# First block's way to its experts on VectorE, second block's front in the head, and a new order table

## The chip, the cores and the metric

The kernel runs on one core of a Trainium2 chip. The time is device microseconds of one execution of the whole program; a median of three runs stands for a kernel. The engines are called as in the profile: PE (matrix products, with PEld for its weight loads), DVE (VectorE), ACT (ScalarE), POOL (GpSimd) and SP, which issues most of the transfers. Each engine works through its own queue in order, and semaphores make it wait for the others.

## The reference

Input is x of 4 sequences with 512 tokens of 256 numbers. Two layers follow, each as x + layernorm(f(layernorm(x))). All numbers are float32.

```python
def _mamba_forward(hidden_states, in_proj_w, conv_w, conv_b, x_proj_w, dt_proj_w, dt_proj_b, A, D, out_proj_w):
    proj = jnp.einsum('bld,ed->ble', hidden_states, in_proj_w)
    x, gate = jnp.split(proj, 2, axis=-1)
    ...
    xc = jax.nn.silu(xc + conv_b[None, :, None])
    ...
    dt = jax.nn.softplus(dt + dt_proj_b)
    def step(state, inp):
        dt_t, x_t, B_t, C_t = inp
        dA = jnp.exp(dt_t[..., None] * A)
        dBx = dt_t[..., None] * B_t[:, None, :] * x_t[..., None]
        state = state * dA + dBx
        y = jnp.einsum('bds,bs->bd', state, C_t)
        return (state, y)
    ...
    y = ys.transpose(1, 0, 2) + xt * D
    y = y * jax.nn.silu(gate)
    return jnp.einsum('bld,ed->ble', y, out_proj_w)
...
    probs = jax.nn.softmax(xt @ w_router, axis=-1)
    top_w, top_i = jax.lax.top_k(probs, TOP_K)
    ...
    g = jax.nn.silu(jnp.einsum('td,edh->teh', xt, we1)) * jnp.einsum('td,edh->teh', xt, we3)
    g = g * cw[:, :, None]
    moe_out = jnp.einsum('teh,ehd->td', g, we2)
    shared = jax.nn.silu(xt @ ws1) * (xt @ ws3) @ ws2
    out = shared / (k + 1) + moe_out * (k / (k + 1))
```

The inner width is 512 with 16 states for each channel; there are 16 experts of width 128, 4 of which are chosen for each token, and a shared one of width 512. All 16 are computed for every token and weighted with `cw`, which is zero for those not chosen.

## The kernel before

The 2048 tokens are cut into 8 blocks of 256 (`N`, `U`); two blocks make a sequence, so an odd block takes over the convolution's tail (`tails`) and the scan's state (`carry`) of the block before it. Each block goes through four stages.

- **front** (L655): statistics of x on DVE (`stats`), 1/deviation on POOL (`rstd`, four small instructions, L380 to L387), normalisation on ACT (`norm`), transposes on PE, copy out of PSUM on ACT (`evict`, giving `xn_t`), the in-projection in two halves (`in`), its copy into a padded tile on ACT (`pad`, with POOL's `pad0` for the three columns before it), the convolution on PE, `sigmoid` on ACT, `silu` on DVE, `x_proj`, `dt`, `softplus`, the products `inputs` on POOL, the gate, and transfers through memory (`rep`, `xg`, `bc`) that spread the results over partitions.
- **scans** (L820): 32 slots for each block (`SLOTS`). A slot is `exps` on ACT (L529), for two slots one `dbx` on POOL (L541), the `scan` on DVE (L824), the product with C on DVE (`hc`, L832), and for four slots one `sum` on PE (L846). After every eight slots `close` (DVE, L858) adds the skip term, and `yg` (POOL, L864) applies the gate. There are three buffers each of `h` (the scan's tile, in PSUM) and `dbx`.
- **chain** (L918): the block's way to its experts: `out0` and `out` (out-projection on PE, L941), `stats1` (DVE), `rstd1` (POOL), `norm1` (ACT), `add1` (POOL, the residual sum, L957), `stats2` (DVE), `rstd2` (POOL), `norm2` (ACT), `turn2` (PE transposes), `evict2` (ACT copy, L974), then the router and the choice of experts.
- **experts** (L1129): ten batches of two experts; the shared one makes the first two. A batch is `h1` and `h3` on PE (L1088, 8 instructions each), `act` on ACT, `gated` on DVE (L1107), `weighted` (L1103, not for the shared one) and `product` (L1110) on POOL, and `down` on PE (L1123). The first may start when `evict2` of its block is done. `fin` to `fstore` normalise, add the residual and store; the last block does it in two halves from PSUM, with the subtraction and the sum on DVE (L1201, L1206).

Block 0's front is written out in `first()` (L545), the head, in a fixed order, while the weights arrive. Idle PE time there is filled with matmuls of the identity (`warm`), which compute nothing. Everything else is a list of tasks, each with its engine, an assumed duration and a rank. `Plan.order()` (L212) makes one order of them by a simulation in which the task with the lowest rank among those that can start is taken next; ranks come from the block and slot, and are moved by the tables `SHIFTS`, `PATIENCE` and `NUDGES`. The order fixes each engine's queue. Where it expects PE to be idle before the first `down`, it puts in `warm` matmuls too. These are the lines of the chain that the change replaces for block 0:

```python
        step("stats1", "DVE", 0.6, stats1, [own("out")], [("mv", own("mv1"))], [own("c1")])
        step("rstd1", "POOL", 1.3, lambda: rstd1(4 * EPS), [own("stats1")], [("rstd", own("rstd1"))], [own("mv1")])
        step("norm1", "ACT", 0.92, norm1, [own("rstd1")], [("o", own("o"))], [own("c1"), own("rstd1")])
        step("add1", "POOL", 1.23, add1, [own("norm1"), own("xr")], (), [own("o"), own("xr")])
        step("stats2", "DVE", 0.615, stats2, [own("add1")], [("mv", own("mv2"))], [own("xr")])
        step("rstd2", "POOL", 1.39, lambda: rstd1(EPS), [own("stats2")], [("rstd", own("rstd2"))], [own("mv2")])
        step("norm2", "ACT", 1.0, norm2, [own("rstd2")], [("xn2", own("xn2"))], [own("xr"), own("rstd2")])
```

Of the kernel before, what the change touches and what calls it, by code (L numbers as in the profile page):

```python
# [57 lines left out]
    fA=(-2, -14.75, -1.5, -59.5, 52, 5.75, 37.75, 15),  # L58
    fB=(20.5, -5, 12.5, 6.25, 26.25, 45.25, 0, -46),
    fC=(7.75, 2, -31, -1.5, 13.5, 14, -33.5, 18),  # L60
    fD=(12, 34.75, 16.5, 0.25, -2.5, 39.25, 8, 11.25),
    exps=(5.75, 36.5, 17.25, -3.75, -60, 51.75, 2, 37.75),
    dbx=(6.5, 1.25, -27.75, -13.5, -14.25, 5.25, 14.25, 46.5),
    scan=(33.75, 18.75, -5.75, 40.75, 52.75, 51.5, 57.25, -15.75),
    hc=(-4.75, -60, 50.25, -27, 28.5, 59.25, 16.75, 26.75),
    keep=(58, 0, -5.75, 0, 52, 0, 14.5, 0),
    sum=(60, -12.75, 1.25, 31.25, 16.5, 7, 0.5, -43.25),
    close=(-4.75, 27.5, 5.5, -13.75, -3, 20, 15, 36.5),
    ld=(1.5, 29.25, 27, -3, 15.75, -7.5, 57.5, -5.25),
    bc=(5, 3, 5.25, 6, 10.5, 15.75, 0.75, -3.25),  # L70
    chain=(-26, -5.25, -55, -60, -6, -38.25, -22.75, 0.25),
    load=(-5.5, 34, -50.25, 21.25, -21.25, -44, 2.75, 5.5),
    h1=(45.5, 3, -35.75, 8.25, 25.75, -0.5, 14.75, 34.5),
    h3=(11.25, -3, -53.5, -26, -29.25, -19, -15.75, -4),
    act=(-6.25, 40.25, 5.5, -11.5, -31.5, 0, 0, -3.25),
    gated=(-2, -9.5, -4.5, -23.25, 11.75, -60, -3, 0),
    prod=(33, -50, 58.75, -60, -50.75, -26.25, -8.75, 0),
    down=(-18.75, 25.5, -45, 42.25, -60, -14, 0.75, 37),
    fin=(14.75, -3, 27.75, 59, 0.5, 59.5, 3.5, -4),
# [3 lines left out]
    fA=(1.5, 0.1, 0.1, 0.3, 0.1, 1, 0.3, 0.1),  # L83
    fB=(2.2, 0.1, 0.1, 0.3, 0.1, 2.2, 0.6, 0.6),
    fC=(0.3, 0.1, 0.3, 1, 0.1, 0.6, 0.3, 0.3),
    fD=(2.2, 0.1, 0.1, 0.1, 0.1, 0.1, 0.1, 0.6),
    exps=(0.1, 0.1, 0.6, 0.1, 1.5, 0.3, 1.5, 0.3),
    dbx=(0.1, 0.3, 0.1, 0.1, 0.1, 0.1, 1, 1.5),
    scan=(0.1, 0.1, 0.1, 0.6, 0.1, 0.1, 0.1, 0.1),
    hc=(0.1, 0.1, 0.6, 1.5, 2.2, 0.1, 2.2, 0.1),  # L90
    keep=(0.1, 0.1, 0.1, 0.1, 0.6, 0.1, 0.1, 0.1),
    sum=(2.2, 0.1, 0.1, 0.1, 2.2, 0.1, 0.1, 0.1),
    close=(0.1, 0.1, 0.6, 1, 0.3, 0.3, 0.6, 1.5),
    ld=(1.5, 0.3, 1.5, 0.3, 0.1, 0.1, 0.1, 1.5),
    bc=(0.6, 0.1, 0.1, 1, 1, 0.1, 0.1, 0.3),
    chain=(0.6, 0.6, 0.1, 0.6, 0.6, 1, 0.1, 2.2),
    load=(2.2, 1, 0.6, 1, 2.2, 2.2, 0.6, 0.1),
    h1=(0.3, 0.3, 0.3, 0.1, 0.1, 0.1, 0.3, 0.1),
    h3=(0.1, 0.3, 2.2, 0.1, 0.1, 1, 0.6, 0.1),
    act=(0.6, 2.2, 0.1, 0.3, 0.1, 0.1, 0.6, 2.2),  # L100
    gated=(0.6, 0.3, 1, 0.1, 0.6, 0.1, 0.1, 1),
    prod=(2.2, 0.1, 0.1, 0.1, 0.1, 0.3, 0.1, 1.5),
    down=(0.1, 0.1, 0.1, 1.5, 0.1, 0.3, 0.1, 0.3),
    fin=(0.3, 0.3, 0.1, 1.5, 0.1, 1, 1, 0.3),
# [3 lines left out]
    ("gin", 0, 0): 5.5, ("pad0", 1, 0): 5.75, ("in", 1, 0): 3, ("xg", 1, 0, 1): 8,  # L108
    ("inputs", 1, 0): 8, ("gate", 1, 0): 14.5, ("evict", 2): 16.5, ("conv", 2, 1): -5.5,
# [41 lines left out]
    close=(CI, "close yg"),  # L151
    ld=(CI, "reps loadxg decay0 decay1 delta"),
    bc=(1, "bc"),
    chain=(1, "xr out0 out stats1 rstd1 norm1 add1 stats2 rstd2 norm2 turn2 evict2 router pads logits "
           "exp choose chosen total share turnw weigh store_cw"),
    load=(NB, "w13 w2 cwb"),
    h1=(NB, "h1"),
# [1168 lines left out]
```

## Time and profile before

| | us |
|---|---|
| median of 3 runs | 694.24 (693.81 to 694.54) |
| the profiled execution | 694.61 |
| its span in the profile | 692.5 |
| busy: PE, DVE, ACT, POOL | 675.8, 578.2, 493.2, 601.6 |
| first scan, last scan ends | 27.89, 613.41 |
| first expert matmul, last `down` ends | 120.16, 687.51 |
| warming matmuls of the order, 164 between 28.0 and 119.9, busy | 21.00 |

The span runs from the program's first instruction to its last; some 2 us of the execution lie around it. Times in views are counted from the start of the span. The first column of a timeline is the start, the second the duration; a bracket tells how long the engine was idle before, and who ended that.

### The profile page before, as it was taken

What the parts mean: (1) busy time and instruction counts of PE and PEld (TensorE: products, weight loads), DVE (VectorE), ACT (ScalarE), POOL (GpSimd) and SP (SyncE); (2) the same over time, 40 slices, a digit from 0 to 9 for tenths busy, and PEclk for the clock granted to TensorE, in tenths of its full rate; (3) what the DMA queues carried; (4) which work ended last, traced back from release to release, by engine and by line L of the source; (5) the groups of instructions that cost most, each with busy time, mean ns of one, the idle gap of its engine ahead of it and who ended that gap; (6) DMA issues with size and microseconds to landing.
All of it is one profiled execution on the core that took longest, in us unless ns stands there. A gap on an engine that the chain in (4) does not pass through costs nothing.

```text
span 692.5 us, 13366 instructions
## 1 busy us (share of the span) xinstructions
PE 675.8 (98%) x4480; PEld 539.9 (78%) x4480; DVE 578.2 (83%) x821; ACT 493.2 (71%) x1308; POOL 601.6 (87%) x607
## 2 busy tenths in 40 slices
PE   8999998999999999999999999999999999999997
PEld 7777776767878678877787787787877787888886
DVE  3698999999999899999999999889999979952112
ACT  2799979988778778877798857877778657733311
POOL 1598669999999999999999999999999999985553
PEclk9999999999999999999999999999999999999999
DMA  5396775586876586788668766688767756464560
GB/s 175 114 352 227 258 238 188 188 270 202 288 230 226 208 307 207 233 264 285 211 227 281 244 221 229 213 290 286 246 240 232 237 190 213 140 227 128 191 229 31
DMA packets 84840, 155.28 MB, mean 224 GB/s; under 512 B 9858, under 2 KB 33410, under 8 KB 84772
## 3 DMA queue, kind: packets, MB, share of 16 engines
q1 hardware_dynamic: 83940, 153.13, 66.3%
q10 hardware_dynamic: 832, 1.31, 0.5%
q8 instruction: 35, 0.57, 0.3%
q14 instruction: 33, 0.27, 0.1%
HBM read 135.40 MB, written 19.01 MB: 223 GB/s over the span
## 4 chain that ended last, share of the span: by engine, by line
PE 62%; DVE 13%; ACT 10%; POOL 8%; DMA 3%; issue 3%; SPq 0%; DVEq 0%; POOLq 0%
PE h L1088 30%; PE po L1123 14%; DVE h L824 7%; PE y L846 6%; POOL dbx L541 4%; ACT h L529 4%; DVE hc L832 3%; PE f L941 3%; PE f L427 2%; PE f L442 2%; DMA xg<-gate 1%; PE f L1123 1%; PE f L349 1%; DVE gate L786 1%; POOL g L1110 1%
## 5 line engine op out<-in xcount | busy, mean ns | idle before, releaser
L824 DVE TENSOR_TENSOR_SCAN h<-h,dbx 128x512 f32<-128x512 f32 x256 | 307.5, 1220 | 11.5 <-ACT h L532 5.9
L541 POOL TENSOR_TENSOR dbx<-rep,bt 128x1024 f32<-128x1024 f32 x127 | 299.7, 2362 | 12.8 <-DVE h L824 12.5
L1088 PE MATMUL h<-xn_t,w 128*128 128x256 f32 x1280 | 295.2, 382 | 0.1
L529 ACT ACTIVATE h<-rep,a_rep 128x256 f32<-128x256 f32 x512 | 244.6, 478 | 53.4 <-DVE hc L832 41.8
L1088 PEld LDWEIGHTS h<-xn_t,w 128*128 128x128 f32 x1280 | 239.5, 190 | 42.7 <-issue 4.0
L832 DVE TENSOR_TENSOR hc<-h,ct 128x512 f32<-128x512 f32 x256 | 170.2, 682 | 2.9 <-ACT carry L836 0.7
L1123 PE MATMUL po<-w,g 128*128 128x256 f32 x600 | 143.6, 382 | 0.8 <-POOL g L1110 0.8
L1123 PEld LDWEIGHTS po<-w,g 128*128 128x128 f32 x600 | 111.8, 190 | 22.0 <-POOL g L1110 3.2
L1110 POOL TENSOR_TENSOR g<-g,q 128x512 f32<-128x512 f32 x80 | 101.6, 1270 | 9.1 <-DVE q L1107 7.1
L1107 DVE SCALAR_TENSOR_TENSOR q<-th,h 128x512 f32<-128x512 f32 x80 | 54.4, 681 | 49.5 <-PE h L1088 41.6
L1103 POOL TENSOR_TENSOR g<-g,cwb 128x512 f32<-128x512 f32 x64 | 81.4, 1271 | 14.6 <-ACT g L1100 13.9
L1095 ACT ACTIVATE th<-h 128x512 f32<-128x512 f32 x80 | 47.5, 594 | 46.8 <-PE h L1088 46.6
L846 PE MATMUL y<-hc,sel 128*32 128x256 f32 x1024 | 67.7, 385 | 0.0
L846 PEld LDWEIGHTS y<-hc,sel 128*32 128x32 f32 x1024 | 27.4, 109 | 28.6 <-issue 14.5
L532 ACT COPY h<-zero 128x1 f32<-128x1 f32 x256 | 41.7, 163 | 8.2
L427 PE MATMUL f<-xn_t,w_in 128*128 128x256 f32 x176 | 42.5, 384 | 1.6 <-DVE gate L786 1.1
L1100 ACT COPY g<-h 128x512 f32<-128x512 f32 x64 | 37.1, 580 | 8.7 <-PE f L1123 8.7
L427 PEld LDWEIGHTS f<-xn_t,w_in 128*128 128x128 f32 x176 | 32.7, 190 | 9.1 <-DVE gate L786 1.7
L836 ACT COPY carry<-h 128x2 f32<-128x2 f32 x128 | 19.6, 159 | 15.4 <-DVE hc L832 7.7
L442 PE MATMUL h<-xp,taps 64*64 64x256 f32 x288 | 29.5, 381 | 0.8 <-DVE xt L459 0.8
L941 PE MATMUL f<-w_out,yg 128*128 128x256 f32 x112 | 26.7, 384 | 0.3 <-DVE xt L459 0.3
L442 PE MATMUL f<-xp,taps 64*64 64x256 f32 x208 | 25.3, 382 | 0.7 <-DVE gate L786 0.4
(178 smaller groups left out, 631.2 us busy)
## 6 DMA issues: line engine op xcount, KB each, us to landing
w<-in_w SPq DMA_DIRECT2D x80, 512.0 KB, 4.4
rep<-rep SPq DMA_DIRECT2D x124, 256.0 KB, 4.6
w<-in_w SPq DMA_DIRECT2D x80, 256.0 KB, 4.5
cwb<-cwd SPq DMA_DIRECT2D x64, 256.0 KB, 5.1
xg<-xg SPq DMA_DIRECT2D x32, 256.0 KB, 4.5
bt<-bc SPq DMA_DIRECT2D x8, 512.0 KB, 5.8
ct<-bc SPq DMA_DIRECT2D x8, 512.0 KB, 6.1
xg<-gate SPq DMA_DIRECT2D x16, 256.0 KB, 4.6
```

Of the source, the lines that this page charges most:

```text
L427: T.matmul(t[:, j, :], w_in[:, k, ts(2 * m + j, P)], q["xn_t", n][:, k, :], start=k == 0, stop=k == CD - 1,)
L442: T.matmul(t[j][half[r ^ j], :], taps[half[r], 2 * m + j, k, :], q["pad", n, m][half[r], j, k : k + U], start=k == 0, stop=k == KC - 1,)
L529: S.activation(h[:, j, :], dt[:, m, 0, :], AF.Exp, scale=a_rep[:, c, g, m : m + 1])
L541: G.tensor_tensor(t[:, m], reps[n * CI + c][:, m, 1, :], bt[:, m], ALU.mult)
L824: V.tensor_tensor_scan(flat, flat, dbx[:, ts(p, NJ), :].rearrange("p j t -> p (j t)"), 0.0, ALU.mult, ALU.add)
L832: V.tensor_tensor(hc, expo[k], ct, ALU.mult)
L846: T.matmul(ys[n, c][m * CS : (m + 1) * CS, :], sel, hcs[k][:, j, :], start=g == 0, stop=g == SG - 1,)
L1088: T.matmul(t[:, j, :], weights[i][:, j, ts(CD * w + k, P)], x[:, k, :], start=k == 0, stop=k == CD - 1,)
L1103: G.tensor_tensor(gs[i], gs[i], cws[i], ALU.mult)
L1107: V.scalar_tensor_tensor(t, hid[i, "th"], 1.0, hid[i, 1], ALU.add, ALU.mult)
L1110: G.tensor_tensor(gs[i], gs[i], hid[i, "q"], ALU.mult)
L1123: T.matmul(acc[n][t] if n == N - 1 else acc[n][:, t, :], gs[i][:, j, ts(t, P)], weights2[i][:, j, :], start=m == 0 and j == 0 and (t == 0 ...
```

## The change

The diff has four parts. Block 0's `close` of the last eight slots leaves its result in PSUM and its `yg` is done on DVE (`quick`). Block 0's chain from `stats1` to `norm2` uses a shorter form: DVE makes the variance plus epsilon beside the statistics (`spread_of`), POOL does the power alone, DVE subtracts the mean in PSUM (`mean1`), scales and adds the residual in one instruction for each half (`scaled1`), and normalises (`scaled2`). The head takes over block 1's front up to the first half of its in-projection, its padding columns, and block 2's statistics; x(1) is asked for earlier, and some of the head's warming matmuls give way to these matmuls. All three tables hold other numbers (only the row of the chain is shown).

```diff
@@ -55,86 +55,83 @@
 SHIFTS = dict(
...
-    chain=(-26, -5.25, -55, -60, -6, -38.25, -22.75, 0.25),
...
+    chain=(-44.5, -50.5, -41.75, -50.75, 13, -21.25, -59.75, -15),
...
@@ -308,6 +305,7 @@
     nc.sync.dma_start(out=chan, in_=a["chan"].rearrange("(c p) k -> p c k", p=P))
+    load_x(1)
     w_x = const.tile([P, CI, P // 2], F32, name="w_x")
@@ -326,8 +324,7 @@
     nc.sync.dma_start(out=bsel, in_=a["bsel"])
-    for n in range(1, 3):
-        load_x(n)
+    load_x(2)
     w_out = const.tile([P, CI, D], F32, name="w_out")
@@ -420,14 +417,20 @@
 
-    def in_proj(n, m, bank):
-        t = q["in", n, m] = ps.tile([P, 2, U], F32, name=bank)
+    def in_parts(n, m, t):
+        q["in", n, m] = t
         for j in range(2):
             for k in range(CD):
                 T.matmul(
                     t[:, j, :], w_in[:, k, ts(2 * m + j, P)], q["xn_t", n][:, k, :],
                     start=k == 0, stop=k == CD - 1,
                 )
+                yield
+    def in_proj(n, m, bank):
+        for _ in in_parts(n, m, ps.tile([P, 2, U], F32, name=bank)):
+            pass
 
@@ -553,6 +556,8 @@
                 xn[:, i, :], xs[0][:, i, :], st[:, i, 1:2], rstd[:, i : i + 1],
                 ALU.subtract, ALU.mult,
             )
+        mr = rstd_of(stats_of(xs[1]))
         xn_t = q["xn_t", 0] = ring(work, [P, CD, U], "xn_t")
         for k, nm in enumerate(("f", "h1")):
             t = ps.tile([P, U], F32, name=nm)
@@ -560,6 +565,8 @@
         make_taps()
+        xn1 = ring(work, [P, NU, D], "o")
+        normalize(xn1, tiles_of(xs[1]), mr)
         for m in range(2):
@@ -571,8 +578,15 @@
             conv(0, m, (("po", "f"), ("h1", "h3"))[m])
+        t = ps_e.tile([P, CD, U], F32, name="h")
+        for k in range(CD):
+            for i in range(NU):
+                T.transpose(t[:, k, ts(i, P)], xn1[:, i, ts(k, P)], ident)
         sigmoid(0, 0)
         silu(0, 0)
+        q["xn_t", 1] = ring(work, [P, CD, U], "g")
+        V.tensor_copy(q["xn_t", 1], t)
 
@@ -580,8 +594,22 @@
         silu(0, 1)
+        live[2]["mv"] = stats_of(xs[2])
+        parts = in_parts(1, 0, ps_e.tile([P, 2, U], F32, name="h"))
+        for m in range(2):
+            xp = q["pad", 1, m] = ring(work, [P, 2, KC - 1 + U], "xp")
+            G.tensor_copy(xp[:, :, 0 : KC - 1], tails.pop((1, m)))
+        def some(c):
+            if c == 1:
+                next(parts)
+                next(parts)
+            else:
+                warm(2, "f")
         S.activation(spare, zero, AF.Softplus)
-        x_proj(0, "y", lambda c: warm(5 - c, "f"))
+        x_proj(0, "y", some)
         ssm(0)
@@ -592,7 +620,9 @@
         V.tensor_copy(first_b, b0)
-        warm(2, "y")
+        for _ in parts:
+            pass
+        V.tensor_copy(q["pad", 1, 0][:, :, KC - 1 :], q["in", 1, 0])
         softplus(0)
@@ -642,6 +672,10 @@
             (), (), [("xt", 0, m)], 256)
+    did(("evict", 1), [("g", ("xn_t", 1))], eng="DVE")
+    for m in range(2):
+        did(("pad0", 1, m), [("xp", ("xp", 1, m))], [("tail", 1, m)], eng="POOL")
+    did(("tail", 1, 0), (), [("xp", 1, 0)], eng="DVE")
     did(("bc", 0), [("bt", ("bt", 0)), ("ct", ("ct", 0))])
@@ -679,12 +713,12 @@
 
-        if n:
+        if n > 1:
             if n > 2:
                 once(key("x"), "SP", 0.5, lambda: load_x(n), (), [("x", key("x"))], (), 256)
 
             def stats():
-                mine["mv"] = stats_of(xs[n])
+                mine["mv"] = live[n].get("mv") or stats_of(xs[n])
 
@@ -714,6 +748,8 @@
 
+        if n:
             def pad0(m):
@@ -727,12 +763,13 @@
 
-            for m in range(2):
+            for m in range(n == 1, 2):
                 ends = (n + 1) % UB
                 starts = n % UB
-                once(key("pad0", m), "POOL", 0.12, lambda m=m: pad0(m),
-                     [("tail", n - 1, m)] if starts else [], [("xp", key("xp", m))],
-                     [("tail", n, m)] if starts else [])
+                if n > 1:
+                    once(key("pad0", m), "POOL", 0.12, lambda m=m: pad0(m),
+                         [("tail", n - 1, m)] if starts else [], [("xp", key("xp", m))],
+                         [("tail", n, m)] if starts else [])
                 banked(key("in", m), 1.73, lambda m=m: in_proj(n, m, bank_of(m)), [key("evict"), key("pad0", m)],
@@ -852,16 +889,25 @@
 
+    def quick(n, c=CI - 1):
+        return n == 0 and c == CI - 1
     def close(n, c):
 
         xg = xgs[n * CI + c]
-        V.scalar_tensor_tensor(xg[:, 0, :], xg[:, 0, :], d_skip[c], ys[n, c], ALU.mult, ALU.add)
+        to = ys[n, c] if quick(n, c) else xg[:, 0, :]
+        V.scalar_tensor_tensor(to, xg[:, 0, :], d_skip[c], ys[n, c], ALU.mult, ALU.add)
 
     def gated_y(n, c):
         xg = xgs[n * CI + c]
         if c % 2 == 0:
             ygs[n, c // 2] = ring(work, [P, 2, U], "yg")
-        G.tensor_tensor(ygs[n, c // 2][:, c % 2, :], xg[:, 0, :], xg[:, 1, :], ALU.mult)
+        if quick(n, c):
+            V.tensor_tensor(ygs[n, c // 2][:, c % 2, :], ys[n, c], xg[:, 1, :], ALU.mult)
+        else:
+            G.tensor_tensor(ygs[n, c // 2][:, c % 2, :], xg[:, 0, :], xg[:, 1, :], ALU.mult)
 
@@ -909,9 +955,10 @@
                     [("sum", s), ("loadxg", i)], (), [("y", i), ("xgt", i)])
-                add(("yg", i), "POOL", 0.685, k - 3 if last else k + 3, lambda n=n, c=c: gated_y(n, c),
+                fast = quick(n, c)
+                add(("yg", i), "DVE" if fast else "POOL", 0.385 if fast else 0.685, k - 3 if last else k + 3, lambda n=n, c=c: gated_y(n, c),
                     [("close", i)] + ([("yg", i - 1)] if i else []),
-                    [("yg", ("yg", n, c // 2))] if c % 2 == 0 else [], [("xgt", i), ("yg", n, c // 2)])
+                    [("yg", ("yg", n, c // 2))] if c % 2 == 0 else [], [("xgt", i), ("yg", n, c // 2)] + ([("y", i)] if fast else []))
 
@@ -925,7 +972,7 @@
             count[0] += 1
-            prev = [(nm, n - 1)] if n else []
+            prev = [(nm, n - 1)] if (nm, n - 1) in plan.names else []
             add((nm, n), eng, dur, base + 0.05 * count[0], fn, list(deps) + prev, alloc, uses, kb)
@@ -948,6 +995,37 @@
             z["mr"] = rstd_of(z["mv"], eps)
+        def spread_of(t):
+            st = z["mv"] = stats_of(t)
+            z["rstd"] = stat.tile([P, NU], F32, name="rstd")
+            V.tensor_scalar(
+                z["rstd"], st[:, :, 2], 1.0 / D, 4 * EPS if t is z["o"] else EPS, ALU.mult, ALU.add
+            )
+        def power():
+            G.tensor_tensor(z["rstd"], z["rstd"], mhalf, ALU.pow)
+        def mean1():
+            for i in range(NU):
+                V.tensor_scalar(z["o"][:, i, :], z["o"][:, i, :], z["mv"][:, i, 1:2], None, ALU.subtract)
+        def scaled1():
+            for i in range(NU):
+                V.scalar_tensor_tensor(
+                    xr[n][:, i, :], z["o"][:, i, :], z["rstd"][:, i : i + 1], xr[n][:, i, :],
+                    ALU.mult, ALU.add,
+                )
+        def scaled2():
+            z["xn"] = ring(work, [P, NU, D], "xn2")
+            for i in range(NU):
+                V.tensor_scalar(
+                    z["xn"][:, i, :], xr[n][:, i, :], z["mv"][:, i, 1:2], z["rstd"][:, i : i + 1],
+                    ALU.subtract, ALU.mult,
+                )
 
@@ -1041,13 +1119,26 @@
              [("yg", n, 1), own("c1")])
-        step("stats1", "DVE", 0.6, stats1, [own("out")], [("mv", own("mv1"))], [own("c1")])
-        step("rstd1", "POOL", 1.3, lambda: rstd1(4 * EPS), [own("stats1")], [("rstd", own("rstd1"))], [own("mv1")])
-        step("norm1", "ACT", 0.92, norm1, [own("rstd1")], [("o", own("o"))], [own("c1"), own("rstd1")])
-        step("add1", "POOL", 1.23, add1, [own("norm1"), own("xr")], (), [own("o"), own("xr")])
-        step("stats2", "DVE", 0.615, stats2, [own("add1")], [("mv", own("mv2"))], [own("xr")])
-        step("rstd2", "POOL", 1.39, lambda: rstd1(EPS), [own("stats2")], [("rstd", own("rstd2"))], [own("mv2")])
-        step("norm2", "ACT", 1.0, norm2, [own("rstd2")], [("xn2", own("xn2"))], [own("xr"), own("rstd2")])
+        if quick(n):
+            step("stats1", "DVE", 0.75, lambda: spread_of(z["o"]), [own("out")],
+                 [("mv", own("mv1")), ("rstd", own("rstd1"))], [own("c1")])
+            step("rstd1", "POOL", 0.71, power, [own("stats1")], (), [own("rstd1")])
+            step("mean1", "DVE", 0.9, mean1, [own("stats1")], (), [own("c1"), own("mv1")])
+            step("add1", "DVE", 0.9, scaled1, [own("rstd1"), own("mean1"), own("xr")], (),
+                 [own("c1"), own("rstd1"), own("xr")])
+            step("stats2", "DVE", 0.75, lambda: spread_of(xr[n]), [own("add1")],
+                 [("mv", own("mv2")), ("rstd", own("rstd2"))], [own("xr")])
+            step("rstd2", "POOL", 0.71, power, [own("stats2")], (), [own("rstd2")])
+            step("norm2", "DVE", 0.75, scaled2, [own("rstd2")], [("xn2", own("xn2"))],
+                 [own("xr"), own("rstd2"), own("mv2")])
+        else:
+            step("stats1", "DVE", 0.6, stats1, [own("out")], [("mv", own("mv1"))], [own("c1")])
+            step("rstd1", "POOL", 1.3, lambda: rstd1(4 * EPS), [own("stats1")], [("rstd", own("rstd1"))], [own("mv1")])
+            step("norm1", "ACT", 0.92, norm1, [own("rstd1")], [("o", own("o"))], [own("c1"), own("rstd1")])
+            step("add1", "POOL", 1.23, add1, [own("norm1"), own("xr")], (), [own("o"), own("xr")])
+            step("stats2", "DVE", 0.615, stats2, [own("add1")], [("mv", own("mv2"))], [own("xr")])
+            step("rstd2", "POOL", 1.39, lambda: rstd1(EPS), [own("stats2")], [("rstd", own("rstd2"))], [own("mv2")])
+            step("norm2", "ACT", 1.0, norm2, [own("rstd2")], [("xn2", own("xn2"))], [own("xr"), own("rstd2")])
         step("turn2", "PE", 0.46, transpose, [own("norm2")],
```

## The prediction

> **What bounds the kernel now.** I read the busy time by stretches first, then the first block's way to its experts in the order of time, then the last block's. The first view gives busy time of PE, PEld, DVE, ACT and POOL in four stretches: the first block's scans, its way to the experts, the long middle until the last scan ends at 613.4, and the rest.
>
> ```profile
> core 0: us, PE busy (x) PEld busy (x) DVE busy (x) ACT busy (x) POOL busy (x), PEclk, DMA share, GB/s
> 28.00:99.00 71.00, 66.58 (x641) 51.50 (x640) 68.36 (x89) 62.09 (x179) 56.26 (x56) 1.00 0.75 250
> 99.00:120.00 21.00, 18.42 (x132) 14.56 (x130) 19.75 (x27) 18.85 (x48) 18.62 (x28) 1.00 0.64 226
> 120.00:613.40 493.40, 490.88 (x3143) 388.26 (x3142) 461.55 (x634) 381.20 (x1024) 479.81 (x460) 1.00 0.71 236
> 613.40:692.50 79.10, 74.11 (x373) 63.84 (x371) 17.04 (x39) 19.09 (x37) 42.58 (x52) 0.98 0.45 151
> ```
>
> Up to 99 DVE sets the pace (96% busy; POOL 79%). In the middle POOL is fullest: 479.81 of 493.40 is 97.2%, idle 13.6 us; DVE 93.5%, idle 31.9 us. PE's 490.88 overstates it, since a matmul of 256 columns is shown as 379 ns but a run of 8 in the chain takes 1.73 us, 216 ns each. After 613.4 only PE matters. So there are two accounts: the last scan's end, which DVE and POOL set, and PE's expert work, which can only begin when the first block has reached its experts.
>
> Block 0's way, instructions in order of time (start, duration):
>
> ```profile
> 99.10 0.47 DVE L858 SCALAR_TENSOR_TENSOR xg<-xg,chan,y 128x256 f32<-128x256 f32 x1
> ...
> 99.64 0.73 POOL L864 TENSOR_TENSOR yg<-xg 128x256 f32<-128x256 f32 x1
> ...
> 102.92 0.69 DVE L377 BATCH_NORM_STATS2 st<-h 128x6 f32<-128x512 f32 x1
> ...
> 105.41 2.35 POOL L541 TENSOR_TENSOR dbx<-rep,bt 128x1024 f32<-128x1024 f32 x1
> 105.75 1.01 ACT L391 ACTIVATE o<-h,off,rstd 128x256 f32<-128x256 f32 x2
> ...
> 107.99 1.28 POOL L957 TENSOR_TENSOR xr<-xr,o 128x512 f32<-128x512 f32 x1
> ...
> 113.61 0.71 POOL L385 TENSOR_TENSOR rstd<-rstd,mhalf 128x2 f32<-128x2 f32 x1
> ...
> 117.71 0.58 ACT L974 COPY xn_t<-h 128x512 f32<-128x512 f32 x1
> ```
>
> From the close at 99.10 to the end of the copy that experts read, 118.29, is 19.2 us; about 7.7 of it is waiting: `add1` sits behind a `dbx` of 2.35, `rstd2` behind a `dbx` and a `u` (110.00 to 113.16). The first expert matmul is at 120.16.
>
> The last block's way:
>
> ```profile
> 618.40 0.48 DVE L858 SCALAR_TENSOR_TENSOR xg<-xg,chan,y 128x256 f32<-128x256 f32 x1 [2.82 <-PE y L846]
> ...
> 631.38 0.59 ACT L974 COPY xn_t<-f 128x512 f32<-128x512 f32 x1
> ...
> 637.27 1.89 PE L1123 MATMUL po<-w,g 128*128 128x256 f32 x8
> ```
>
> At 631.97, when block 7's experts may begin, PE has of block 6 only the rest of one `down` (1.2 us) and one whole (1.73): 2.9 us. So PE can arrive at most 2.9 us earlier before it waits for the last scans; more must come from a sooner end of the scans.
>
> **The head.** Added on DVE: statistics of x(1) and x(2), 0.69 each (L377), and two copies of 128x512 from PSUM, 0.69 each (L569 on DVE). On POOL four small ones, 0.19+0.22+0.71+0.20 = 1.3, and two tail copies of 0.19. On ACT two normalisations, 1.1. On PE four transposes, 0.55, and `in` of block 1, 1.73, for 4+2 warming matmuls. Covers: ACT stood idle 2.08 before 11.81; POOL stood idle 15.5 before 22.92; DVE 3.4 before 22.41 (x(2) statistics) and 1.2 before 24.07 (the pad copy). Without its cover each would cost its own length. Not covered is the copy of `xn_t` 1: it stands on DVE between the two `silu`, which run without a gap (16.95 to 19.01). It pushes the second by 0.69; the matmuls behind started at 19.34 though their data was there by 18.6 and 19.0, so 0.3 is absorbed: **+0.4 us**, bounds 0 and 0.8.
>
> x(1) is now asked for behind `chan`, at about 1.6 on SP's queue, not 8.03; w_x, one_row, w_dt, a_rep, rsel and bsel move back by one issue and 256 KB. Its statistics are ahead of DVE's copy of `xn_t` 0 at 9.57, so a late landing would hold the head. w_x, issued at that very place, landed at 8.02, and x(1) is wanted at 8.1; it is twice the bytes in half as many rows. I take 0, keep 1.5 us as the upper bound. w_x is wanted only at 17.49.
>
> **Block 0's scans.** Two statistics leave DVE (one stood at 27.27, straight before the first scan): -1.4. With the head +0.4 the close comes 1.0 earlier. POOL loses rstd of block 1 and two pads, 1.3+0.4; ACT normalisation, copy and pad, 2.3; PE 2.3.
>
> **The way itself.** Work, by rows: close 0.40 (pipelined), `yg` on DVE 0.45 (nearest L858), out 1.56, statistics 0.69 and a 128x2 step 0.17 (nearest the reciprocal, 166 ns), power on POOL 0.71, subtraction of the mean beside it, scale and add 0.87 (the pair L1206 at 688.87 to 689.74), statistics and step 0.86, power 0.71, two normalising steps 0.74 (L552), transposes 0.55, copy 0.58: 8.6, and nine crossings of some 0.1: 9.5. Waits that the row cannot show: power behind a `dbx` 0 to 2.36, twice; four times a scan of 1.22 ahead on DVE; once exps on ACT, 0 to 1. Together 0 to 10.6. I take 3.0, nearer the low end, because a power of 0.71 has two small gaps to hit where before three POOL steps had to be fitted. Way: **12.5 instead of 19.2, -6.7** (bounds -9.7 and +0.9). Experts begin 7.7 earlier.
>
> DVE pays for it: 0.45 + 2x0.17 + mean 0.85 (pair L1201) + 0.87 + 0.74 = 3.25, and behind them in its queue stand block 1's scans, for which exps and `dbx` buffers wait. POOL sheds yg 0.73, add 1.27, six small ones 1.2: 3.2. ACT sheds 2.1.
>
> The Trainium skill, "SBUF — State Buffer", Who interferes with whom, speaks against the last of these steps: a `tensor_scalar` from SBUF to SBUF may take a two-port mode, and then DVE and GpSimd lock each other out for a whole instruction. L552, which has that form, ran at 410 ns beside an idle POOL, so no row here shows the lock; by the rule one step could wait for a whole `dbx`, the way would be 2.4 longer, and PE's account below would give 2.6 and bind: 691.6.
>
> **PE's account.** Experts 7.7 earlier; but in 110.4 to 118.3 PE did real work of two `in` (3.46), transposes 0.55 and one `sum` 1.0, some 5.0, which is now later; 2.3 went into the head. 7.7 - 5.0 + 2.3 = 5.0 earlier, if nothing else binds.
>
> **The scans' end.** By POOL: 3.2 + 1.7 less work, +0.4: -4.5. By DVE: +3.25 - 1.4 + 0.4: +2.3. POOL is the fuller in the middle, but DVE before it; two thirds to one: **-2.3**. Of the 2.9 us left over one `down` goes: **-1.7**. Sum **-4.0**. PE's 5.0 allows it.
>
> **The new table** changes every engine's order. Seven blocks of 32 scans with nearly the same work started 71.5, 73.0, 76.2, 75.2, 74.6, 70.6 and 75.0 us apart (standard deviation 2.1); over seven independent ones that is 2.1 x 2.65 = 5.5. I take 0 for it and keep 5.5 both ways.
>
> The span was 692.5 and that execution 694.61, 0.37 above the median of 694.24: 688.5 of span, 690.6 for that execution, 690.2 for a median.
>
> **Rivals.** (1) DVE sets the scans' end (+2.3) and the leftover 2.9 gives it back: 694.24 - 0.6 = 693.6. For it: DVE 96% up to 99 and every new step on DVE; against it: 31.9 us idle later, where 3 could sink. (2) Slower: in the middle, the new order leaves DVE idle for more than its 6.5%. Each point is 4.9 us on the scans' end. It decides from where the last scan ends over 2.9 later than 613.4; at one point more, 4.9 + 2.3 - 2.9 = 4.3: 698.5. For it: the spread of the blocks; against: POOL's relief. (3) The way isn't shortened since the two powers meet `dbx` each time: only the relief and the head remain, DVE's price stays, about 694.2. (4) A long gain: POOL rules and all leftover goes, -4.5 - 2.9: 686.8.
>
> **Chances.** Forecast 0.48 (its own range 687.5 to 692.8), (4) and better 0.17, (1) 0.12, (3) 0.07, (2) 0.16. About 0.2% (1.4 us) is what a measurement can tell from no change. Faster: 0.48 + 0.17 + 0.05 of (1) = 0.70. Same: 0.05 of (1), 0.05 of (3) = 0.10. Slower: 0.16 and 0.04 of the rest = 0.20. Range: -4.0 less 5.5 is 684.7; above, it must reach into (2) with a bit under half of it: 697. I take 684.5 to 697.
>
> **What would show it.** Right: close to copy of block 0 within 11 to 15 us; the copy's end near 110.5; first scan near 27.7 (0.69 saved, 0.4 lost); last scan near 611; after 632 PE with one `down` of block 6 or none. Wrong: the in-projection of the head after 10.5 (x(1) late); the last scan after 615 with DVE over 95% busy (rival 1) or under 93% (rival 2); expert matmuls still from 117 on (rival 3).

## The result and the profile after

The changed kernel takes 699.69 us (median of 4 runs, 699.15 to 699.81), beside 694.20 for the kernel before: ratio 1.0076, interval 1.0064 to 1.0088. It is slower by 5.5 us, outside the range of 684.5 to 697.0. Its span is 697.9, 5.4 more.

| us | before | after | forecast |
|---|---|---|---|
| first scan starts | 27.89 | 26.88 | 27.7 |
| block 0's last close starts | 99.10 | 103.15 | 98.1 |
| from there to the end of the copy `evict2` | 19.19 | 12.93 | 12.5 |
| that copy ends | 118.29 | 116.08 | 110.5 |
| first expert matmul | 120.16 | 119.63 | 112.5 |
| last scan ends | 613.41 | 620.29 | 611.1 |
| block 7's copy `evict2` ends | 631.97 | 638.58 | 629.7 |
| last `down` ends | 687.51 | 692.60 | 683.5 |

The last column is the value of before with the prediction's terms. The first view is the busy time of the engines in the same four stretches as before: block 0's scans, its way, the middle up to the last scan, the rest.

```profile
core 0: us, PE busy (x) PEld busy (x) DVE busy (x) ACT busy (x) POOL busy (x), PEclk, DMA share, GB/s
27.00:103.10 76.10, 69.96 (x668) 53.44 (x666) 71.38 (x90) 66.06 (x186) 58.94 (x55) 0.98 0.73 247
103.10:119.60 16.50, 15.35 (x116) 11.88 (x114) 16.19 (x35) 14.83 (x36) 12.60 (x17) 1.00 0.70 242
119.60:620.30 500.70, 495.72 (x3139) 389.69 (x3136) 465.03 (x634) 380.25 (x1023) 483.22 (x462) 1.00 0.70 232
620.30:697.90 77.60, 72.30 (x365) 62.32 (x363) 15.63 (x36) 17.97 (x35) 39.84 (x47) 0.98 0.45 153
```

Block 0's scans have become 5.1 longer (76.1 for 71.0), the way shorter, the middle 7.3 longer with about the same number of instructions on each engine (DVE 634 both times, POOL 462 for 460), the rest 1.5 shorter. About half of the middle's 7.3 is longer busy time (DVE 465.03 for 461.55, POOL 483.22 for 479.81), the other half idle time that the other order leaves. DVE is 92.9% busy there (465.03 of 500.70; 93.5% before). The way in the order of time, all engines:

```profile
103.15 0.46 DVE L901 SCALAR_TENSOR_TENSOR y<-xg,chan,y 128x256 f32<-128x256 f32 x1
...
104.12 0.41 DVE L908 TENSOR_TENSOR yg<-y,xg 128x256 f32<-128x256 f32 x1
...
107.63 0.17 DVE L1004 TENSOR_SCALAR rstd<-st 128x2 f32<-128x2 f32 x1
...
107.88 0.70 POOL L1009 TENSOR_TENSOR rstd<-rstd,mhalf 128x2 f32<-128x2 f32 x1 [0.50 <-DVE rstd L1004]
...
109.94 2.38 POOL L544 TENSOR_TENSOR dbx<-rep,bt 128x1024 f32<-128x1024 f32 x1
...
111.85 0.48 DVE L1004 TENSOR_SCALAR rstd<-st 128x2 f32<-128x2 f32 x1
...
112.54 0.69 POOL L1009 TENSOR_TENSOR rstd<-rstd,mhalf 128x2 f32<-128x2 f32 x1
...
113.98 0.70 DVE L1025 TENSOR_SCALAR xn<-xr,st,rstd 128x256 f32<-128x256 f32 x2
...
115.50 0.58 ACT L1052 COPY xn_t<-h 128x512 f32<-128x512 f32 x1
```

The way is as short as forecast. One line does not fit: the same 128x2 step takes 0.17 at 107.63, where POOL is idle, and 0.48 at 111.85; there it ends 0.02 after the `dbx` of POOL (112.337 and 112.314 in the trace). More on this below. In the last block:

```profile
623.58 0.48 DVE L901 SCALAR_TENSOR_TENSOR xg<-xg,chan,y 128x256 f32<-128x256 f32 x1 [2.18 <-PE y L883]
...
637.79 1.89 PE L1214 MATMUL po<-w,g 128*128 128x256 f32 x8
637.99 0.59 ACT L1052 COPY xn_t<-f 128x512 f32<-128x512 f32 x1 [2.31 <-PE f L1049]
```

When block 7's copy ends at 638.58, PE is in the last `down` of block 6; nothing whole is left over, as forecast. The copy comes 6.6 later, as the scans do (6.9), and the last `down` 5.1 later.

From a block's first scan to the next block's (in block 7 to the end of its last scan) it is, blocks 0 to 7: before 69.3, 71.5, 73.0, 76.2, 75.2, 74.6, 70.6, 75.0; after 74.0, 69.3, 73.9, 72.8, 73.6, 74.1, 71.2, 84.6. The loss is in block 0 (+4.7) and block 7 (+9.6); the six between won 6.2 back. In block 7 the order has put more of the experts' work beside the scans. The same view for that block, before and then after:

```profile
535.00:613.40 78.40, 78.40 (x457) 63.77 (x456) 70.85 (x97) 52.47 (x139) 76.39 (x78) 1.00 0.60 199
```

```profile
535.70:620.30 84.60, 84.60 (x486) 69.21 (x485) 72.00 (x96) 54.09 (x138) 81.11 (x84) 1.00 0.64 210
```

POOL does 84 instructions instead of 78 in the same scans, 4.7 us more, and PE 486 matrix products instead of 457, while DVE does about the same (1.2 more).

**Plan and chip.** `Plan.order()` of the kernel gives every task a start. Run by itself it ends at 665.2 for before and 668.6 for after, and plans block 7 at 75.1 and 84.7. So 3.4 of the 5.4 are in the plan that the new table makes; that the code does not force them is seen below, where the same code with another table is planned at 662.5 (`c_after`). Below, "drift" is the start of the i-th scan in the profile less that of the i-th scan in the plan. It begins with the head (some 27, the plan's zero), and where it grows, the chip does something that the plan did not count. The runs named in the table are told further down.

| drift at scan | 1 | 17 | 33 | 49 | 256 |
|---|---|---|---|---|---|
| before | 27.3 | 27.8 | 28.7 | 28.8 | 28.4 |
| after | 26.3 | 29.0 | 30.6 | 30.4 | 30.4 |
| `e_scan1` | 26.8 | 28.0 | 29.5 | 29.3 | 29.1 |
| `c_before` | 27.1 | 27.8 | 28.7 | 28.6 | 28.6 |
| `c_after` | 27.1 | 27.3 | 29.0 | 31.5 | 33.1 |
| `f_after` | 27.3 | 27.5 | 29.2 | 31.9 | 34.0 |
| `n_after` | 27.4 | 27.6 | 29.3 | 29.6 | 32.0 |

From the 33rd scan on, the drifts of before and of after in this table stay within 0.4 us (between the scans listed they swing by up to 1.3). After loses 2.7 in the first 16 scans, where before loses 0.5. The 5.4 is made up of the plan (+3.4), the start (-1.0), the opening (+2.2) and the rest (+0.8).

### The profile page after: what moved, and what is told of

It is laid out like the page before. It is cut to its first block, busy times and chain, and to the rows that moved or that the text cites. A ratio compares the mean times of both kernels' runs of the same rounds, so it can differ in the third digit from the quotient of the medians.

```text
span 697.9 us, 13365 instructions
## 1 busy us (share of the span) xinstructions
PE 678.5 (97%) x4474; PEld 538.3 (77%) x4474; DVE 581.6 (83%) x832; ACT 491.5 (70%) x1302; POOL 600.3 (86%) x599
## 4 chain that ended last, share of the span: by engine, by line
PE 55%; ACT 14%; DVE 14%; POOL 7%; issue 4%; DMA 4%; SPq 0%; DVEq 0%; POOLq 0%; ACTq 0%
PE h L1179 26%; PE po L1214 13%; ACT h L532 7%; DVE h L861 7%; PE y L883 4%; DVE hc L869 4%; POOL dbx L544 4%; DMA rep<-rep 2%; PE f L425 2%; PE f L988 2%; PE f L1214 1%; PE f L346 1%; DVE q L1198 1%; POOL g L1201 1%; ACT h L535 1%
## 5 line engine op out<-in xcount | busy, mean ns | idle before, releaser
L883 PEld LDWEIGHTS y<-hc,sel 128*32 128x32 f32 x1024 | 27.3, 109 | 30.6 <-issue 15.1
L425 PE MATMUL f<-xn_t,w_in 128*128 128x256 f32 x160 | 38.7, 385 | 0.5 <-ACT carry L873 0.4
L425 PEld LDWEIGHTS f<-xn_t,w_in 128*128 128x128 f32 x160 | 29.6, 190 | 7.7 <-issue 1.6
```

Source lines behind the costliest of these rows:

```text
L425: T.matmul(t[:, j, :], w_in[:, k, ts(2 * m + j, P)], q["xn_t", n][:, k, :], start=k == 0, stop=k == CD - 1,)
L883: T.matmul(ys[n, c][m * CS : (m + 1) * CS, :], sel, hcs[k][:, j, :], start=g == 0, stop=g == SG - 1,)
```

## The experiments

**1. No table, and each other's.** Tables emptied in four codes (before; after; only the short way, with the head of before; only the head, with `quick` off), then the two tables exchanged. Theory T: the code gains and the table loses; theory C: the code itself costs.

```diff
-SHIFTS = dict(fA=..., ...)
+SHIFTS = {}
+PATIENCE = {}
+NUDGES = {}
...
     def quick(n, c=CI - 1):
-        return n == 0 and c == CI - 1
+        return False
```

> The kernel before with its three order tables emptied, so that ranks alone make the order. It is the base for the next three. Both theories: slower than 694.2, between 705 and 740, since the tables hold what was found by search. No part of the computation changes.

> The changed code with empty tables. Theory T (the code is a gain, the new table is a worse order): 2 to 6 us below the kernel before with empty tables; experts begin 5 us or more earlier. Theory C (the code itself costs: VectorE has 3 us more before the experts and block 0 is held up): equal to it or up to 8 us above.

> Only the short way of block 0 (close, yg and chain on VectorE), the old head, empty tables. T: the way from close to the copy that experts read is 6 us shorter than with the long way, and the time 1 to 5 us below the kernel before with empty tables. C: the way is shorter too, but the scans end later by 3 us or more and the time is above.

> Only the new head (block 1's front begun there, x(1) earlier), the long way of block 0, empty tables. T: the first scan some 1 us earlier as in the changed kernel (26.9 against 27.9), time 1 to 3 us below the kernel before with empty tables. C: no gain or above it.

> The code of after with the table of before: the change without its table. Theory T (a table fits one code only, and its worth is lost when the list of steps changes): far from both, 730 to 745 us, the way of block 0 still short. Rival (the old table was the better one as such): 688 to 695.

> The code of before with the table of after: the new table alone. T: far from both, 730 to 745 us. Rival (the new table is worse by itself, by some us): 697 to 702.

Measured: before 736.05, after 737.8, short way alone 739.57, head alone 728.07 (ratios 1.0604, 1.063, 1.0655, 1.049, each within 0.0026). The code of after with the old table 740.58, the code of before with the new one 740.4 (1.0673, 1.0656, within 0.0022). A table carries some 40 us and fits one code only: with the other code it is no better than none, as T had it. So no run shows the change with the table left as it was. Of the codes without a table, the short way (3.5 above) and the whole change (1.8 above) lie in C's windows, while the head brings 8.0, more than T has. The single orders are uneven (one block of 102.7 us in one run, one of 104.5 in another, and the four times of before without a table lie between 733.69 and 738.12), so these four don't settle the sign.

**2. The same search for each code.** A table was searched from nothing, by random steps that lower the planned end, 1500 s with one seed for each of the four codes.

> The code before with a table found from nothing by one search of 1500 s, the same search with the same seed for each of four codes; its goal is the end that the kernel's own planner reckons with. It plans 678 us here, where the table that the kernel came with plans 665 and ran in 694.2. Both theories: some 28 to 33 above the plan, 706 to 711 us. It is the mark for the other three.

> The code after with a table from the same search (planned 669). Theory T (the code gains, the change's own table lost it): well below the code before with its searched table, by 4 us or more, 696 to 703. Theory C (the code itself costs time in any order): not below it, 706 us or more. The way from close to the copy of block 0 should be some 13 us by both.

> Only the short way of block 0, with the head of before, and a table from the same search (planned 676). T: 0 to 5 us below the code before with its searched table, 703 to 709. C: above it by the VectorE work of 3.2 us that the way adds, 709 to 714.

> Only the new head, with the way of before, and a table from the same search (planned 675). T: 2 to 7 us below the code before with its searched table, 700 to 707. C, in the form that the new head is what costs: above it.

| | planned | measured | ratio (interval) |
|---|---|---|---|
| before | 678.2 | 711.98 | 1.0260 (1.0245 to 1.0275) |
| after | 668.9 | 707.64 | 1.0188 (1.0171 to 1.0205) |
| short way alone | 676.3 | 710.71 | 1.0240 (1.0220 to 1.0260) |
| head alone | 674.9 | 708.26 | 1.0201 (1.0186 to 1.0216) |

The code of after is 4.3 below that of before, the short way 1.3 and the head 3.7, the differences that T has. All four times lie above T's windows, and those of after and of the short way are times that C gave; and with one search for each code, a part of the differences can be luck of the search. The plan promised 9.4 for after, and 5.0 of it were lost on the chip: after lies 38.8 above its plan, before 33.8. The drift of `s_after` goes from 26.5 to 32.9 within 16 scans, that of `s_before` from 26.5 to 30.5.

**3. The opening of the scans.** The first scans of after, DVE and POOL in the order of time:

```profile
26.88 1.22 DVE L861 TENSOR_TENSOR_SCAN h<-h,dbx 128x512 f32<-128x512 f32 x1
27.04 1.27 POOL L544 TENSOR_TENSOR dbx<-rep,th 128x512 f32<-128x512 f32 x1 [0.46 <-DVE rep L640]
28.14 0.69 DVE L869 TENSOR_TENSOR hc<-h,ct 128x512 f32<-128x512 f32 x1
28.27 0.73 POOL L644 TENSOR_TENSOR u<-dt,xt 128x256 f32<-128x256 f32 x1
28.97 2.35 POOL L544 TENSOR_TENSOR dbx<-rep,bt 128x1024 f32<-128x1024 f32 x1
28.98 0.69 DVE L823 SCALAR_TENSOR_TENSOR gate<-sig,f 128x512 f32<-128x512 f32 x1 [0.16 <-ACT sig L819]
...
31.35 1.23 DVE L861 TENSOR_TENSOR_SCAN h<-h,dbx 128x512 f32<-128x512 f32 x1 [1.68 <-POOL dbx L544]
```

DVE stands idle 1.68 before its second scan. That scan is slot 2's, whose `dbx` POOL ends at 31.32. Slot 1's, ready since 28.3, is queued behind it: the new table moves slot 1's scan later (`("scan", 1): 10.25`). The planner can't see the price, because it counts the second `dbx` as done at its zero (`did(("dbx", i), ...)` without an end). The kernel before sends slots 0 and 1 first and does not wait (two scans in a row):

```profile
27.89 2.33 DVE L824 TENSOR_TENSOR_SCAN h<-h,dbx 128x512 f32<-128x512 f32 x2
```

The edit touches the finished order alone (`move` puts its first task right behind its second):

```diff
-    for t in plan.order():
+    order = plan.order()
+    move(("scan", 2), ("hc", 1))
+    move(("keep", 2), ("keep", 1))
+    for t in order:
```

> The code and the table of after; in the finished order the scan of slot 2 alone moves behind the scan of slot 1 and its product, and slot 2's small carry copy on ScalarE behind slot 1's. Theory D (the planner counts the second dbx as done at its zero, while GpSimd ends it at 31.3; the new table therefore sends slot 2's scan to VectorE second, and VectorE stands 1.68 us there): the idle at 29.67 goes, all later scans come 1.2 to 1.7 us earlier, 698.0 to 698.5 us. Rival (something later in the first block takes the gain back: GpSimd's own wait at 43.6, or the loads of the first block): 699.4 to 700.0.

Measured 698.32 (1.0053, 1.0040 to 1.0067), 1.4 below after. Theory D is right, in size too. The scan at 30.14 is now slot 1's, that at 32.01 slot 2's:

```profile
27.43 1.22 DVE L861 TENSOR_TENSOR_SCAN h<-h,dbx 128x512 f32<-128x512 f32 x1
...
30.14 1.22 DVE L861 TENSOR_TENSOR_SCAN h<-h,dbx 128x512 f32<-128x512 f32 x1
31.40 0.69 DVE L869 TENSOR_TENSOR hc<-h,ct 128x512 f32<-128x512 f32 x1
...
32.01 1.22 DVE L861 TENSOR_TENSOR_SCAN h<-h,dbx 128x512 f32<-128x512 f32 x1
```

None of these scans waits any more.

**4. The planner told the truth, and both codes searched on.** POOL's part of the head and the second `dbx` (in the code of after SP's part too) get the ends that the profile shows, and the search goes on from each kernel's own table. The cut shows the code of after; `c_before` has 5.6 and 4.4 and was searched for as long as the last leg of `c_after` only.

```diff
-    BUSY = dict(POOL=5.35, ACT=0.35, SP=6.0)
+    BUSY = dict(POOL=6.2, ACT=0.35, SP=7.6)
-        did(("dbx", i), [("dbx", ("dbx", i))], [("rep", 0), ("bt", 0)], eng="POOL")
+        did(("dbx", i), [("dbx", ("dbx", i))], [("rep", 0), ("bt", 0)], eng="POOL", end=5.1 * i)
```

> The code of after; the planner is told that GpSimd ends its part of the head 6.2 us after its zero (not 5.35), SyncE 7.6 (not 6.0) and the second dbx at 5.1 (not 0); the table is searched on from after's own one with that. Planned 662.5. Theory T (code gains, the change's own table and the planner's blind spot lost it): zero at 26.9 with 0.5 to 1.5 of drift as in the code before, span 690 to 691.5, 691.7 to 693.3 us, faster than before by 0.9 to 2.5. Theory C (the code itself costs beyond what its planner counts): drift of 2 to 5 on top, 694.5 to 698.

> As c_after with the table of a second search (another seed), planned 662.9. T: 692.1 to 693.7. C: 695 to 698.5. Against c_after it shows what two tables of one plan differ by on the chip: by T under 1.5 us.

> The code of before; the planner is told of GpSimd 5.6 and the second dbx 4.4; the table is searched on from before's own one in the same way and for as long as the last leg of c_after. Planned 664.1, where the table of before has 665.3. T: 692.8 to 693.8, 0.5 to 1.5 above c_after. C: below c_after.

Measured: `c_after` 696.48 (1.0039, 1.0026 to 1.0051), `c_after2` 696.86 (1.0039, 1.0026 to 1.0053), `c_before` 693.40 (0.9991, 0.9982 to 0.9999). T falls in this form: the code of after has the better plan (662.5 for 664.1) and is 3.1 slower. `c_after` and `c_after2` lie in C's windows: this code costs something that its planner does not count. In `c_after` the opening is now right (27.3 at the 17th scan), but between the 33rd and 49th the drift grows by 2.5. That is block 0's way. There, in `c_after`:

```profile
108.28 2.37 POOL L2813 TENSOR_TENSOR dbx<-rep,bt 128x1024 f32<-128x1024 f32 x1
...
108.50 0.69 DVE L2643 BATCH_NORM_STATS2 st<-xr 128x6 f32<-128x512 f32 x1
...
109.23 1.45 DVE L3273 TENSOR_SCALAR rstd<-st 128x2 f32<-128x2 f32 x1
...
113.60 2.35 POOL L2813 TENSOR_TENSOR dbx<-rep,bt 128x1024 f32<-128x1024 f32 x1 [1.90 <-DVE h L3130]
114.02 2.40 DVE L3294 TENSOR_SCALAR xn<-xr,st,rstd 128x256 f32<-128x256 f32 x2
```

The step of 0.17 takes 1.45 and ends at 110.68, 0.03 after the `dbx` (110.65). The pair of 0.70 takes 2.40: its first half, 2.07 long, ends at 116.09, after a `dbx` that ends at 115.95. In all that is 2.98 more than these steps take beside an idle POOL. Below, such a step is called held; the profile shows the hold as a longer instruction, not as idle time. A semaphore doesn't do that: a step of 0.17 that is let go at 110.65 ends at 110.82 at the earliest. In `c_after2` the first half of the pair starts at 113.14, before the `dbx`, and takes 0.39; the second starts behind it and takes 2.43:

```profile
113.14 2.74 DVE L3300 TENSOR_SCALAR xn<-xr,st,rstd 128x256 f32<-128x256 f32 x2
113.32 2.42 POOL L2819 TENSOR_TENSOR dbx<-rep,bt 128x1024 f32<-128x1024 f32 x1 [1.06 <-DVE h L3136]
```

In all nine runs that have these steps in this form, each one that started under a `dbx` or a `u` with more than 0.2 us still to go ended 0.02 to 0.14 us behind it (under a power of 128x2 one pair did not wait), and none of `mean1`'s (L1013 of after), which read and write PSUM, was held: 0.48 and 0.49 each time. What was lost so, summed over a run: 0.3 in after and `e_scan1`, 1.0 and 1.9 in the two without a table, 2.0 in `s_quick`, 3.0 and 3.1 in `c_after` and `c_after2`, nothing in the other two. At the last scan `c_after` has drifted 4.5 more than `c_before` (33.1 and 28.6); the 1.6 by which it grows behind the 49th scan is not explained.

**5. Another form of the same steps.** If the name `tensor_scalar` is what is held, `scalar_tensor_tensor` should run through.

```diff
-            V.tensor_scalar(
-                z["rstd"], st[:, :, 2], 1.0 / D, 4 * EPS if t is z["o"] else EPS, ALU.mult, ALU.add
+            V.scalar_tensor_tensor(
+                z["rstd"], st[:, :, 2], 1.0 / D, eps1 if t is z["o"] else eps2, ALU.mult, ALU.add
...
-                V.tensor_scalar(
-                    z["xn"][:, i, :], xr[n][:, i, :], z["mv"][:, i, 1:2], z["rstd"][:, i : i + 1],
-                    ALU.subtract, ALU.mult,
+                V.scalar_tensor_tensor(
+                    z["xn"][:, i, :], xr[n][:, i, :], z["mv"][:, i, 1:2],
+                    z["rstd"][:, i : i + 1].to_broadcast([P, D]), ALU.subtract, ALU.mult,
```

> c_after with the three SBUF-to-SBUF tensor_scalar groups of block 0's way written as scalar_tensor_tensor (the eps from a small tile, rstd broadcast along the row), in the same order. Theory L (a tensor_scalar from SBUF to SBUF on VectorE is held until GpSimd's running instruction ends; 1.28 + 1.68 us were lost so in c_after): the three steps take 0.17, 0.17 and 0.85 us beside the same dbx, the drift at the 40th scan is 28.5 to 29.2 instead of 31.8, and 693.5 to 694.3 us instead of 696.5. Rival W (GpSimd or a busy memory slows any VectorE step there): the steps stay at 1 to 2.5 us, 696 to 697.

> c_after2 with the same edit; 1.07 + 2.04 us were held there. L: 693.7 to 694.6 instead of 696.9, with about 2 us of c_after2's later drift still there. W: 696.4 to 697.4.

Measured 698.12 (1.0055, 1.0042 to 1.0067) and 697.25 (1.0045, 1.0031 to 1.0059): theory L misses; the second time lies in W's window, the first above it. The steps are held as before:

```profile
108.43 2.37 POOL L2817 TENSOR_TENSOR dbx<-rep,bt 128x1024 f32<-128x1024 f32 x1
...
109.37 1.44 DVE L3277 SCALAR_TENSOR_TENSOR rstd<-st,eps 128x2 f32<-128x2 f32 x1
...
114.17 2.60 DVE L3298 SCALAR_TENSOR_TENSOR xn<-xr,st,rstd 128x256 f32<-128x256 f32 x2
```

W falls too: block 0's close and `scaled1`, which have this very form, took 0.46 to 0.49 a piece wherever they ran under a `dbx` or `u`. They read one operand from PSUM; so do `scan` and `hc` (their `h` lies in PSUM), `gated` and `silu`. But taking everything from SBUF is not enough to be held. The statistics of `xr` do so and ran their 0.69 under the same `dbx` of `c_after` (108.50 above); over all runs, 150 statistics of `x`, `xr` and `res` that began under a `dbx` or `u` which outlasted them took 0.67 to 0.71, and 62 reciprocals of 128x2 took 0.17. Held were two forms: `tensor_scalar` from SBUF to SBUF, and `scalar_tensor_tensor` with two tensors in SBUF.

The Trainium skill, "SBUF — State Buffer", Who interferes with whom, has both cases. It was cited in the prediction for the first, the two-port mode of `tensor_scalar`. It also says that a VectorE instruction with two inputs in SBUF contends with a GpSimd instruction that reads SBUF, which is what this edit made. The trace agrees with both as far as the hold goes (1.45 for 0.17 in the one form, 1.44 for 0.16 in the other; in which mode the first form ran, it does not show), and with the page's word that the one that issues first decides (0.39, then 2.43).

**6. Nothing from SBUF to SBUF.** The same order; the 128x2 steps go to POOL ahead of the power, and the residual sum stays in PSUM until ACT copies it.

```diff
+            G.tensor_scalar(z["rstd"], z["mv"][:, :, 2], 1.0 / D, eps, ALU.mult, ALU.add)
             G.tensor_tensor(z["rstd"], z["rstd"], mhalf, ALU.pow)
...
-                    xr[n][:, i, :], z["o"][:, i, :], z["rstd"][:, i : i + 1], xr[n][:, i, :],
+                    z["o"][:, i, :], z["o"][:, i, :], z["rstd"][:, i : i + 1], xr[n][:, i, :],
...
-                    z["xn"][:, i, :], xr[n][:, i, :], z["mv"][:, i, 1:2], z["rstd"][:, i : i + 1],
+                    z["xn"][:, i, :], z["o"][:, i, :], z["mv"][:, i, 1:2], z["rstd"][:, i : i + 1],
...
+            S.copy(xr[n], z["o"])
```

> c_after in the same order, with no SBUF-to-SBUF step on VectorE left in block 0's way: the two 128x2 steps stand on GpSimd ahead of the powers (0.19 each, with 0.09 between), the sum of the residual stays in its PSUM bank, its statistics and its normalisation read it there, and ScalarE copies it to SBUF (0.58). Theory P (a VectorE step that takes its operands from SBUF alone is held until GpSimd's running instruction ends; one with an operand in PSUM is not): the normalising steps take 0.49 each beside a dbx, the drift at the 40th scan falls from 31.8 to 28.9 to 29.6, and 693.3 to 694.3 us instead of 696.5. Rival W (any new step there costs that, or GpSimd's queue takes it back): drift 31 or more, 695.5 to 697.

Measured 695.47 beside 694.63 (1.0010, 1.0001 to 1.0019; `c_after` had 1.0039). The drift at the 49th scan is 29.6 instead of 31.5, the steps run through under a `dbx`:

```profile
112.84 2.36 POOL L2813 TENSOR_TENSOR dbx<-rep,bt 128x1024 f32<-128x1024 f32 x1
113.26 0.99 DVE L3291 TENSOR_SCALAR xn<-h,st,rstd 128x256 f32<-128x256 f32 x2
```

That is what theory P has for the steps (0.53 a piece for its 0.49) and for the drift; the time is 1.2 above its window, at the edge of W's. Of P's wording only the half on PSUM is shown: the statistics above speak against the other half. By the ratios 2.0 of the 3.0 held came back. The steps in PSUM are longer by 0.45 (1.02 and 0.99 for 0.85 and 0.70), and from the 49th scan to the last the drift grows by 2.4, where `c_after` has 1.6; why is open.

**7. Searched on once more.** `n_after`'s code with a table of another 4000 s (planned 660.9 for 662.5).

> n_after's code (no step of block 0's way held) with a table searched on for another 4000 s, planned 660.9 where n_after's table has 662.5. If the plan carries over as it did in c_before (0.6 to 1.2 less planned, 0.6 less measured), 1.6 less than n_after: 693.0 to 694.4, ratio 0.997 to 1.000. Rival (what the plan doesn't count in this code eats it, as in c_after): 694.8 to 696.

Measured **691.98** (691.87 to 692.46) beside 694.27: ratio 0.9971, 0.9959 to 0.9983. It is faster than both kernels, by 2.3 and 7.7 us; the ratio is at the good end of what was expected, the time 1.0 below it. The code of before was not run with as long a search; the run with the shorter one, `c_before`, gives 693.40, so the part of these 2.3 that the code earns, and the part that the longer search earns, is not settled.

## Why the prediction was wrong

**What held.** The way: 12.93 for 12.5. That is in good part luck: its 3.0 of waiting was picked out of 0 to 10.6, the work listed adds up to 8.3 and not to 8.6, and the same steps took 17.1 in `c_after` and 17.7 in `c_after2` (3.0 and 3.1 of it held), 11.0 in `s_after` and 23.3 in the changed code without a table. The way's length, too, is set by the order. The leftover: no whole `down` of block 6 when block 7's copy ends, and the last `down` ends 5.1 later where the scans end 6.9 later, 1.8 less for the 1.7 said (the rest of a `down` at 631.97 was 0.9, not 1.2: it began at 630.97 and took 1.89). x(1) was not late (the in-projection starts at 9.11). The head: the last copy of `rep`, behind which the scans begin, ends at 26.90 in the mean of 7 profiles with the old head (standard deviation 0.34) and at 27.30 in 13 with the new (0.29): +0.4 as said, known to some 0.15. The profile of after alone (first scan 1.0 earlier) would have told otherwise; there a statistics of 0.6 ahead of the first scan has gone as well.

**The step that failed: "I take 0" for the new table.** The miss lies wholly in the scans' end, 6.9 later where 2.3 earlier was said. The table's term had bounds of ±5.5, from the spread of the blocks, and it came out at +3.4 in the plan and +1.4 for the opening wait, 4.8 in all. A table is worth some 40 us and was found for one list of tasks. The list changed, so the old gain was gone and a new one had to be found; nothing in the prediction made it likely that it would be as good, and it did not use the plan's own end, which shows the 3.4. That 4.8 lies within the 5.5 is luck, since nothing ties the spread of the blocks in one order to what another order costs. Rival 2, "in the middle, the new order leaves DVE idle", which had 0.16, came by its signs (last scan 6.9 later, DVE under 93%), and only in part by its mechanism: DVE's idle time in the middle rose from 31.9 to 35.7, 3.8 of the 6.9, and block 0's scans, 5.1 longer, are in no rival. That 699.69 is near its 698.5 is luck as well.

**"The scans' end", -2.3, did not follow from work.** From the first scan to the last, DVE is busy 552.7 for 549.8, and POOL 554.7 for 554.8; the forecast had 3.25 - 1.4 = 1.85 more for DVE and 4.9 less for POOL. 2.7 of POOL's relief went into experts' work that the order did ahead of the last scan: behind it POOL has 39.84 of work left, not 42.58, DVE 15.63, not 17.04. Idle time on both grew, to 40.7 (35.7) and 38.7 (30.7). POOL's busy time stayed and the end still moved by 6.9: here the order set that end, not the sum of busy times.

**Block 0's close "1.0 earlier" came 4.05 later.** The wait at the opening is 1.68 of it. The rest is other work that the order put among block 0's scans (DVE 90 instructions for 89, but 71.38 us for 68.36), and idle time.

**"PE's account", 5.0 earlier, was never drawn on.** The experts began 0.5 earlier, not 7.7: the close was late, and PE took a `conv` between router and first expert. The scans' end binds, since nothing of block 6 is left over; what a shorter way is worth by itself was not measured with tables searched long.

**The rule that was weighed and set aside.** The prediction costed the hold at 2.4 for one step and took none, since the one row of that form (L552) ran beside an idle POOL. In after it costs only 0.31, because both powers and the last step met a free POOL; so it is not why this kernel is slower. In `c_after` it is 3.0, more than the whole gain of its plan (662.5 for 665.2).

## What to carry to other kernels

When a change comes with a new order or schedule, price the order as its own term: look whether the planner's own end falls, and whether its picture of the start is true, ahead of adding up durations. A drift between plan and trace, taken at each task of one kind, shows at once where the chip does what the plan does not know. And before a step moves to VectorE beside a busy GpSimd, ask for its form and where its operands lie. In these runs a `tensor_scalar` or `scalar_tensor_tensor` with an operand in PSUM ran through; with all of them in SBUF, one that came behind the start of a `dbx` (some 2.4 us) or a `u` waited for its end. Statistics and reciprocals from SBUF did not wait.

## What was not expected of the hardware

A VectorE step of 0.17 us took up to 1.77 (the short way without a table), and a half of 0.40 up to 2.43, beside one GpSimd instruction of 2.36; the GpSimd instruction itself grew little (2.42 and 2.49 where one such step was under way at its start). Thirteen executions of the new head ended between 26.95 and 27.97, as their first statistics began between 5.17 and 6.73: a head of one profile says little about a change of 0.4.
